# Lending the scan's PSUM banks, keeping a weight for two groups, and opening with zeros, in a two-layer kernel planned by a list scheduler

## The chip, the cores and the metric

The kernel runs on one core of a Trainium2 chip. The metric is the device time of one execution in microseconds (us). Three executions of the kernel before took 1812.67, 1815.26 and 1815.69 us, so the median is 1815.26 us. Everything is computed in float32.

The core has five engines that run their own instruction streams and meet at semaphores. In the profile PE is TensorE (matmuls; PEld is its loading of the stationary operand), DVE is VectorE, ACT is ScalarE, POOL is GpSimd, and SP only issues DMA transfers. A q behind an engine's name (SPq, POOLq, ACTq) is its instruction queue, most often while it issues a DMA.

## The reference

Two layers, each a sequence mixer and a feed-forward net (FFN), work on 2048 tokens of 512 features, with a residual and a layer norm behind every part:

```python
x = _layernorm(x + _L0_attn_ref(x, ...))   # chunked linear attention, 16 heads, decay per head
x = _layernorm(x + _L0_ffn_ref(x, ...))    # silu(x W1') * (x W3'), Walsh-Hadamard transform, W2'
x = _layernorm(x + _L1_attn_ref(x, ...))   # selective scan, 32 states a channel
x = _layernorm(x + _L1_ffn_ref(x, ...))    # silu(gate) * up, down projection

# L0 attention: q, k, v = silu(x Wq), silu(x Wk), silu(x Wv); per chunk of 128 tokens:
scores = einsum(qb, kb) * D                # D: decay by distance, causal
o = einsum(scores, vb) + einsum(qb, S) * q_decay
S = chunk_decay * S + einsum(kb * k_decay, vb)
# then sigmoid gate, RMS norm by head, Wo
# L1 scan over time, for each channel d and state n:
h = exp(delta_t * A) * h + (delta_t * u_t) * B_t;  y_t = sum_n h * C_t;  y + u * D_param
```

## The kernel before

**Groups and phases.** The tokens are worked in five groups (`GROUPS`): 256 tokens, three times 512, and 256. `PHASES` lists the work of the groups: `V0`..`V4` are the value products of the attention (`front`), `A0`..`A4` the rest of the attention (`attention`), `F0`..`F4` the first layer's FFN, and `f0, a1, b1, f2, f3, f4` the second layer's FFN. Between `F` and the small-letter phases lies the group's selective scan (class `Scan`). `F0`, `f0`, `a1` and `b1` (the phases named in `FILLERS`) run as fillers behind other work.

**Who sets the order.** Nothing is reordered by a compiler: the context is traced under a manual schedule. The class `Order` is a list scheduler that runs while the program is built. Every piece of work is an `Op` with an engine, a modelled duration, the buffers it reads and writes, the tagged buffers it takes and those it gives back. Each phase is a thread (a Python generator) that yields ops. `Order.run` takes for every engine the op that can begin first, with ties broken by a priority, and issues it. So each engine's instruction order is fixed by the model, and on the chip each engine follows that order and waits at semaphores. A thread can also yield a condition (`yield lambda: ...`); it goes on once that holds in the model.

**PSUM.** The eight banks are split for the whole run. Tag `mm` is four buffers of one bank, which all products, transposes and accumulations take in turn. Tag `da` is two buffers of two banks, which only the scan uses: ACT writes exp(delta A) there (L1412), DVE runs the scan in place (L1440) and multiplies by C (L1453).

**Weights.** `load_weights` streams all weights through a ring of 16 buffers of 256 KB each on SP's queue, in the order `PLAN`. Every phase takes its own pieces (`take`), so `Wv` is loaded once for each of the five groups. At piece 12 (3\*EB) and piece 28 (7\*EB) the stream stops until two, and then four, of the 1 MB quarters of W2 (`w2f`) have been requested. `transformed_w2` requests them; DVE and PE transform them and `w2h` in DRAM takes the result, which `F` phases read.

**The start.** `load_first` issues on SP: the identity matrix (needed by PE's transposes), the first group's two chunks of x, and then spawns the constants' loads (`load_consts`, all on POOL's queue, the decay parameters `ld` among the first), the weights and W2. Group 0: transposes (L527), copies out of PSUM (ACT, L534), value products (L607), q and k products (L658) in two blocks, gates (L677).

**The attention of later groups.** In `attention`, `projections` (the q and k products, L658) begin for groups 1 to 4 only when every chunk's values have been through their silu in the model (L970). The silu runs on ACT (L501), which must load another activation table (1.28 us, ACT_TABLE_LOAD) when it comes from exp or log work.

**The scan.** `Scan.inputs` transposes the group, and the product with W_bc (L1254) and the dt product (L1271) follow. `Scan.decays` issues the exps on ACT into `da`, `Scan.steps` the scans on DVE; `products` and `sums` run on POOL and by accumulating DMAs. Group after group: a scan begins its exps once the one before has issued its own.

Of the kernel before, what the change touches and what calls it, by code (L numbers as in the profile page):

```python
# [16 lines left out]
P = 128  # L17
# [25 lines left out]
FILLERS = {"F0": (), "f0": ("F0", "F1"), "a1": ("f0", "F2"), "b1": ("a1", "F3")}  # L43

PLAN = (
    "V0 A0 V1 A1:8 F0:8 A1 F0 F1 V2 A2:8 f0:8 A2 f0 F2 V3 A3:8 a1:8 A3 a1 F3 V4 A4:8 b1:8 A4 b1 "
    "F4 f2 f3 f4"
).split()

# [26 lines left out]
        self.r, self.w, self.a, self.free, self.spare = r, w, a, free, spare  # L76


class Order:


# [16 lines left out]
        self.now = 0.0  # L98

    def tag(self, name, n, make):  # L100
        self.tags[name] = (n, make, [])

    def spawn(self, gen, prio=0):
        self.new.append([gen, prio, None])
# [1 line left out]
    def begin(self, op, spare=True):  # L106

        t = self.free[op.eng]
        for b in op.r:
            if b.written is None:  # L110
                return None
            t = max(t, b.written + self.HOP)
        for b in op.w:
            t = max(t, b.last + self.HOP)
        for name in {name for name, _ in op.a}:
            n, _, bufs = self.tags[name]
            k = sum(name == v for v, _ in op.a) + (op.spare if spare else 0) - (n - len(bufs))
            if k > 0:
                free = sorted(b.last for b in bufs if b.refs <= 0)
                if len(free) < k:  # L120
                    return None
                t = max(t, free[k - 1] + self.HOP)
        return t

    def switches(self, op):
# [2 lines left out]

    def put(self, op, t):
        for name, b in op.a:  # L130
            n, make, bufs = self.tags[name]
            if len(bufs) == n:
                bufs.remove(min((v for v in bufs if v.refs <= 0), key=lambda v: v.last))
            b.t = make()
            bufs.append(b)
# [77 lines left out]
def two_layers(  # L213
# [15 lines left out]
    ps = ctx.enter_context(tc.tile_pool(name="ps", bufs=4, space=PSUM))  # L229
# [11 lines left out]
    def tagged(name, n, pool, shape):  # L241
        order.tag(name, n, lambda: pool().tile(shape, F32, tag=name, name=name, bufs=n))

    tagged("mm", 4, lambda: ps, [P, 512])
    tagged("da", 2, lambda: ps, [P, 2, G])
    tagged("xT", 2, lambda: gp, [P, EB * G])
    tagged("xf", 1, lambda: gp, [P, EB * G // 2])
    tagged("h", 10, lambda: gp, [P, G])
# [80 lines left out]
    def plan():  # L329
        for ph in PHASES:  # L330
            mine = of_phase[ph] = []
            if ph[0] in "VA":
                for w in (wv,) if ph[0] == "V" else (wq, wk, wo):
                    mine.extend((v, Buf(), ()) for v in rows_of(w, 0, EB))
                continue
            if ph[0] == "F":
                wg, wu, u0, wd, needs = w1t, w3t, 0, w2h, w2h_b
            else:
                wg, wu, u0, wd, needs = wgut, wgut, FF, wdnt, ()
            r0 = 0  # L340
# [7 lines left out]
        at = dict.fromkeys(PHASES, 0)  # L348
# [6 lines left out]
        assert all(at[ph] == len(of_phase[ph]) for ph in PHASES)  # L355

    def load_weights():
        for i, (src, b, needs) in enumerate(pieces):
# [59 lines left out]
    ident_b, consts_b, decays_b, scan_b, early_b, hadamard_b = (Buf() for _ in range(6))  # L418

    def load_first():  # L420
        nc.vector.memset(one, 1.0)
        nc.vector.memset(eps, EPS)
        nc.vector.memset(eps4, 4.0 * EPS)
        yield dma(KB256 / 4, lambda: ident, lambda: consts[:, C_ID : C_ID + P], w=[ident_b])
        yield from load_x(0)
        spawn(load_consts())
        spawn(load_weights())
        spawn(transformed_w2())

    def load_consts():  # L430
        yield dma(
            65536, lambda: early[:, 0, :], lambda: consts[:, C_H : C_H + P], eng="POOL",
            w=[hadamard_b],
        )

        yield dma(8192, lambda: ldb, lambda: ld.partition_broadcast(P), eng="POOL")
        for j in range(HPB):
            yield dma(
                512, lambda: ldp[j * HD : (j + 1) * HD, :],
                lambda: ld.rearrange("(k j) -> j k", j=HPB)[j].partition_broadcast(HD),  # L440
                allow_slow_non_contiguous=True, eng="POOL",
            )
        for j, c0 in ((1, C_DIFF), (2, C_MASK), (3, C_IDX)):
            yield dma(
                65536, lambda: early[:, j, :], lambda: consts[:, c0 : c0 + P],
                w=[early_b] if j == 3 else [], eng="POOL",
            )
        yield dma(
            4096, lambda: cst[:, 2 * P :], lambda: consts[:, C_REV : C_HM + 4],
            allow_slow_non_contiguous=True, eng="POOL",  # L450
        )
        yield dma(65536, lambda: blk, lambda: consts[:, C_BLK : C_BLK + P], eng="POOL")
        yield dma(65536, lambda: wg1_s, lambda: wg1.rearrange("(k p) e -> p k e", p=P), eng="POOL")
        for k in range(EB):
            yield dma(
                65536, lambda: wg2_s[k * HD : (k + 1) * HD, :], lambda: wg2, eng="POOL"
            )
# [167 lines left out]
    def attention(gi, nxt, prio):  # L625
# [341 lines left out]
        def projections():  # L967
            if gi:

                yield lambda: all(b.written is not None for b in v2)  # L970
            for vb in range(VB):
                for j in range(2):
                    yield from project(j, vb)
                if vb == 0:
                    yield from gates()
            reached(f"A{gi}")
# [236 lines left out]
    class Scan:  # L1213
# [189 lines left out]
        def decays(self):  # L1403
            if self.gi:
                yield lambda: scans[self.gi - 1].decayed
            U = len(self.units)
            for i, (n, k0) in enumerate(self.units):
                da, delta = self.da[i], self.delta[k0 // self.W]
# [19 lines left out]
        def steps(self):  # L1428
# [3 lines left out]
            for i, (n, k0) in enumerate(units):  # L1432
# [227 lines left out]
```

## Time and profile before

| what | value |
|---|---|
| median of three executions | 1815.26 us |
| the profiled execution's own span, first to last instruction | 1815.4 us |
| mean granted TensorE clock over it | 0.988 |
| PE busy | 1771.1 us (98%) |
| DVE, ACT, POOL busy | 1282.1, 1163.7, 1096.7 us |
| HBM traffic over the span | 152 GB/s |
| first and last exp of a scan (L1412) | 289.2 and 1663.3 us |
| transfers of 256 KB of Wv, median issue to landing | 20, 5.0 us |

The page gives each engine's busy time, the span in 40 slices, the chain of work that ended last, and the costliest groups. The waits view lists, for each line, whom it waited for: total, times, longest. The timeline gives one row for each merged run of instructions: start, duration, engine, line, what it writes and reads, count, and in brackets the idle time of the engine before it with what ended that idle time. The windows view gives, for each stretch, the busy time of the engines (in brackets their instructions), then the mean granted TensorE clock, the busy share of the DMA engines and GB/s.

### The profile page before, as it was taken

How to read it: one execution, taken by the hardware profiler on the slowest of the kernel's cores; microseconds unless marked ns; L12 is line 12 of the kernel's file. 1: busy time of each engine (PE TensorE's matmuls, PEld its weight loads, DVE VectorE, ACT ScalarE, POOL GpSimd, SP SyncE). 2: the span in 40 equal slices, each digit the busy share in tenths (PEclk: the TensorE clock that was granted, in tenths of full speed). 3: DMA queues.
4: the chain of work that ended last, by engine and by line, in shares of the span. 5: the costliest groups of instructions: out<-in, count | busy, mean ns of one | idle time of the engine just before them, and what ended most of it. 6: DMA issues, size and time to landing. Idle time of an engine off the chain costs nothing.

```text
span 1815.4 us, 21241 instructions
## 1 busy us (share of the span) xinstructions
PE 1771.1 (98%) x7064; PEld 1004.1 (55%) x7064; DVE 1282.1 (71%) x1537; ACT 1163.7 (64%) x1832; POOL 1096.7 (60%) x595
## 2 busy tenths in 40 slices
PE   8999999998999999999999999999999999999998
PEld 5456764443467644444666444676865444544574
DVE  3643115987599899944899999539999899998211
ACT  3734046688876676869767767686766868775311
POOL 2000015887577899935779989337998998776000
PEclk9999999999999999999999999999999999999999
DMA  9542435766648778745587787467989874766251
GB/s 283 156 139 82 151 118 168 197 164 175 210 128 253 206 207 233 200 119 185 154 221 221 199 231 212 143 213 236 275 241 262 204 213 159 199 172 168 81 174 58
DMA packets 225421, 336.32 MB, mean 185 GB/s; under 512 B 19569, under 2 KB 128897, under 8 KB 225313
## 3 DMA queue, kind: packets, MB, share of 16 engines
q1 hardware_dynamic: 206192, 270.86, 47.2%
q0 software_dynamic: 16816, 59.92, 17.6%
q10 hardware_dynamic: 2304, 4.20, 0.6%
q8 instruction: 56, 0.92, 0.2%
q14 instruction: 53, 0.43, 0.1%
HBM read 253.12 MB, written 22.54 MB: 152 GB/s over the span
## 4 chain that ended last, share of the span: by engine, by line
PE 67%; DVE 10%; ACT 8%; DMA 7%; POOL 4%; issue 3%; SPq 1%; DVEq 0%; POOLq 0%
PE mm L1052 36%; PE mm L1106 17%; DVE da L1440 6%; PE mm L658 4%; DMA y<-dbu 4%; POOL dbu L1392 3%; PE mm L1003 2%; ACT da L1412 2%; DVE dbu L1453 2%; PE mm L607 2%; ACT L501 1%; ACT L1412 1%; PE mm L845 1%; PE mm L1254 1%; PE mm L936 1%
## 5 line engine op out<-in xcount | busy, mean ns | idle before, releaser
L1392 POOL TENSOR_TENSOR dbu<-du,B 128x1024 f32<-128x1024 f32 x256 | 649.6, 2561 | 124.2 <-DMA y<-dbu 92.8
L1052 PE MATMUL mm<-xT,w 128*128 128x512 f32 (+1 forms) x1912 | 668.1, 510 | 2.9 <-ACT h L501 2.5
L1052 PEld LDWEIGHTS mm<-xT,w 128*128 128x128 f32 x1912 | 363.6, 191 | 303.9 <-issue 266.3
L1412 ACT ACTIVATE da<-delta,a_s 128x512 f32<-128x512 f32 (+1 forms) x640 | 384.4, 605 | 148.2 <-DVE dbu L1453 117.7
L1440 DVE TENSOR_TENSOR_SCAN da<-da,hlast,dbu 128x512 f32<-128x512 f32 (+1 forms) x384 | 425.8, 1109 | 36.9 <-ACT da L1412 27.7
L1489 POOL TENSOR_TENSOR y<-y,dbu 128x1024 f32<-128x1024 f32 x123 | 323.6, 2631 | 55.2 <-DVE dbu L1453 49.7
L1106 PE MATMUL mm<-w,h 128*128 128x512 f32 x768 | 339.4, 595 | 3.5 <-DMA w<-w2h 1.8
L1453 DVE TENSOR_TENSOR dbu<-da,C 128x1024 f32<-128x1024 f32 x256 | 312.9, 1222 | 13.9 <-ACT hlast L1465 7.0
L1440 DVE TENSOR_TENSOR_SCAN da<-da,dbu 128x256 f32<-128x256 f32 (+1 forms) x256 | 246.0, 961 | 26.7 <-ACT da L1412 18.8
L1106 PEld LDWEIGHTS mm<-w,h 128*128 128x128 f32 x768 | 145.2, 191 | 177.2 <-issue 164.4
L1052 PE MATMUL mm<-xf,w 128*128 128x256 f32 x1024 | 231.2, 385 | 0.2 <-DVE sc L863 0.2
L1052 PEld LDWEIGHTS mm<-xf,w 128*128 128x128 f32 x1024 | 196.7, 194 | 33.2 <-issue 4.6
L501 ACT ACT_TABLE_LOAD x143 | 183.5, 1283 | 5.1 <-PE mm L1052 2.3
L501 ACT ACTIVATE h<-mm 128x512 f32<-128x512 f32 x144 | 85.7, 597 | 114.3 <-PE mm L1052 66.3
L1083 DVE TENSOR_TENSOR h<-h,mm 128x512 f32<-128x512 f32 x96 | 65.2, 679 | 111.2 <-PE mm L1052 105.7
L1412 ACT ACT_TABLE_LOAD x109 | 139.8, 1283 | 1.9
L658 PE MATMUL mm<-xT,w 128*128 128x512 f32 (+1 forms) x320 | 116.6, 513 | 3.8 <-DVE sc L863 1.3
L299 POOL DMA_DIRECT2D y<-dbu x113 | 109.1, 966 | 12.4 <-DMA y<-dbu 5.1
L1465 ACT COPY hlast<-da 128x2 f32<-128x2 f32 (+1 forms) x160 | 25.4, 159 | 141.0 <-DVE dbu L1453 120.5
L1106 PE MATMUL mm<-w,hf 128*128 128x512 f32 x256 | 112.8, 592 | 0.0
L748 POOL TENSOR_TENSOR qd<-h,q_dec 128x512 f32<-128x512 f32 x14 | 17.8, 1271 | 151.0 <-ACT h L501 83.0
L1125 DVE TENSOR_TENSOR xn<-mm,xn 128x512 f32<-128x512 f32 x60 | 40.9, 681 | 92.9 <-PE mm L1106 92.5
(100 smaller groups left out, 1358.2 us busy)
## 6 DMA issues: line engine op xcount, KB each, us to landing
y<-dbu POOLq DMA_DIRECT2D x113, 512.0 KB, 6.0
w<-in_wgut_dram SPq DMA_DIRECT2D x192, 256.0 KB, 4.6
B<-rows SPq DMA_DIRECT2D x128, 256.0 KB, 4.6
C<-rows SPq DMA_DIRECT2D x128, 256.0 KB, 4.2
w<-in_wdnt_dram SPq DMA_DIRECT2D x96, 256.0 KB, 4.8
w<-in_w1t_dram SPq DMA_DIRECT2D x80, 256.0 KB, 4.7
w<-in_w3t_dram SPq DMA_DIRECT2D x80, 256.0 KB, 5.0
w<-w2h SPq DMA_DIRECT2D x80, 256.0 KB, 4.2
```

What stands on the lines that cost most here:

```text
L299: return Op(eng, us, lambda: of.dma_start(dst(), src(), **more), dma=nbytes, **kw)
L501: nc.scalar.activation(dst, src, AF.Silu)
L658: nc.tensor.matmul(bank.t[:, s * T : (s + 1) * T], w_qk[j][k].t[:, eb * P : (eb + 1) * P], xT.t[:, k, :], start=k == 0, stop=k == EB - 1,)
L1052: nc.tensor.matmul(bank.t[:, s * T + c0 * P : s * T + c1 * P], blocks[fb // 2][j][k // 2].t[:, k % 2 * 2 * P + k0 : k % 2 * 2 * P + k0 + P ...
L1083: 512, lambda: nc.vector.tensor_mul(t.t, t.t, pu.t), r=[pu], w=[t], free=[pu]
L1106: nc.tensor.matmul(accs[c].t, hT[f // S].t[:, s * T + c * P : s * T + (c + 1) * P], w_d[f].t, start=f == 0, stop=f == nt * S - 1,)
L1125: nc.vector.tensor_add(xb.t, bank.t, xb.t)
L1392: 1024, lambda: nc.gpsimd.tensor_mul(self.wide(self.db[i]), self.wide(du), self.row(self.bs, i)),
L1412: nc.scalar.activation(d[:, j, :], self.wide(delta)[:, j, :], AF.Exp, scale=a_s[:, k0 + j, n : n + 1],)
L1440: nc.vector.tensor_tensor_scan(d()[:, j, :], d()[:, j, :], self.wide(db)[:, j, :], init, ALU.mult, ALU.add,)
L1453: 1024, lambda: nc.vector.tensor_mul(self.wide(db), d(), self.row(self.cs, i)),
L1489: 1024, lambda: nc.gpsimd.tensor_add(y.t, y.t, db[i].t), r=o, w=[y],
```

## The change

The change has four parts, all in the planned program.

1. **Banks.** PSUM is now two tiles of four banks, and a new class `Banks` hands out single banks (`mm`) or aligned pairs (`da`) by when they come free. While no scan is open, `mm` may take all eight; while one is open it may take banks 0 to 3. A scan opens when its first `delta` load has been issued in the model and the scan before has issued its exps; it closes when its last multiplication has been issued.
2. **Wv for two groups.** `V1` leaves `PLAN`, and group 1 uses group 0's four buffers of Wv, which are held for both. The stop at piece 28 now falls behind four pieces of `F0`.
3. **The start.** DVE clears `dp1` (128x512), and PE multiplies zeros: one product of 512 and one of 256 columns at the very start, and one of 512 columns after the loads of x. The identity is issued on ACT's queue instead of SP's. The five small loads of `ld` go behind the gate weights in POOL's queue.
4. **q and k.** The condition at L970 becomes one that always holds, so q and k products no longer stand behind the values' silu.

```diff
 PLAN = (
-    "V0 A0 V1 A1:8 F0:8 A1 F0 F1 V2 ..."
+    "V0 A0 A1:8 F0:8 A1 F0 F1 V2 ..."
...
+class Banks:
+    def __init__(self, views, usable):
+        self.views, self.usable = views, usable
+        self.holders = [None] * 8
+    def free_at(self, i):
+        b = self.holders[i]
+        return -1.0 if b is None else b.last if b.refs <= 0 else None
...
+class BankTag:
+    def places(self):
+        f, out = self.banks.free_at, []
+        for i in self.banks.usable(self.width):
+            at = [f(j) for j in range(i, i + self.width)]
+            if None not in at:
+                out.append((max(at), i))
+        return sorted(out)
...
-    tagged("mm", 4, lambda: ps, [P, 512])
-    tagged("da", 2, lambda: ps, [P, 2, G])
+    halves = [ps.tile([P, 4, G], F32, name=name) for name in ("mm", "da")]
+    opened = set()
+
+    def usable(width):
+        if width == 2:
+            return (4, 6)
+        return range(4 if opened else 8)
...
+            if ph == "V1":
+                for v, b, needs in of_phase["V0"]:
+                    b.refs += 1
+                    mine.append((v, b, needs))
+                continue
...
     def load_first():
+        nc.vector.memset(dp1, 0.0)
...
-        yield dma(KB256 / 4, lambda: ident, lambda: consts[:, C_ID : C_ID + P], w=[ident_b])
+        spawn(warming(3.0, (512, 256)))
+        yield dma(
+            KB256 / 4, lambda: ident, lambda: consts[:, C_ID : C_ID + P], eng="ACT", w=[ident_b]
+        )
         yield from load_x(0)
+        spawn(warming(0.9, (512,)))
...
+    def warming(us, cols):
+        bank = Buf()
+        def mm():
+            for n in cols:
+                nc.tensor.matmul(
+                    bank.t[:, :n], dp1[:, :P], dp1[:, :n], start=True, stop=True
+                )
+        yield pe(us, mm, a=[("mm", bank)], free=[bank])
...
     def load_consts():
...
-        yield dma(8192, lambda: ldb, lambda: ld.partition_broadcast(P), eng="POOL")
-        for j in range(HPB):
-            yield dma(512, lambda: ldp[j * HD : (j + 1) * HD, :], ..., eng="POOL")
...
         for k in range(EB):
             yield dma(65536, lambda: wg2_s[k * HD : (k + 1) * HD, :], lambda: wg2, eng="POOL")
+        yield dma(8192, lambda: ldb, lambda: ld.partition_broadcast(P), eng="POOL")
+        for j in range(HPB):
+            yield dma(512, lambda: ldp[j * HD : (j + 1) * HD, :], ..., eng="POOL")
...
         def projections():
             if gi:
-                yield lambda: all(b.written is not None for b in v2)
+                yield lambda: True
...
         def decays(self):
             if self.gi:
                 yield lambda: scans[self.gi - 1].decayed
+            yield lambda: self.delta[0].written is not None
+            opened.add(self.gi)
...
             self.stepped = True
+            opened.discard(self.gi)
```

More of the change, by code (lines that the diff above doesn't have):

```diff
@@ L45 @@
 PLAN = (
-    "V0 A0 V1 A1:8 F0:8 A1 F0 F1 V2 A2:8 f0:8 A2 f0 F2 V3 A3:8 a1:8 A3 a1 F3 V4 A4:8 b1:8 A4 b1 "
+    "V0 A0 A1:8 F0:8 A1 F0 F1 V2 A2:8 f0:8 A2 f0 F2 V3 A3:8 a1:8 A3 a1 F3 V4 A4:8 b1:8 A4 b1 "
     "F4 f2 f3 f4"
@@ L76, in __init__, with when, take, of @@
         self.r, self.w, self.a, self.free, self.spare = r, w, a, free, spare
+class Tiles:
+    def __init__(self, n, make):
+        self.n, self.make, self.bufs = n, make, []
+    def when(self, k):
+        k -= self.n - len(self.bufs)
+        if k <= 0:
+            return -1.0
+        free = sorted(b.last for b in self.bufs if b.refs <= 0)
+        return free[k - 1] if len(free) >= k else None
+    def take(self, b):
+        if len(self.bufs) == self.n:
+            self.bufs.remove(min((v for v in self.bufs if v.refs <= 0), key=lambda v: v.last))
+        b.t = self.make()
+        self.bufs.append(b)
+class Banks:
[5 more added lines that the diff above has]
+        return -1.0 if b is None else b.last if b.refs <= 0 else None
+    def of(self, width):
+        return BankTag(self, width)
+class BankTag:
+    def __init__(self, banks, width):
+        self.banks, self.width = banks, width
+    def places(self):
[5 more added lines that the diff above has]
+        return sorted(out)
+    def when(self, k):
+        free = self.places()
+        return free[k - 1][0] if len(free) >= k else None
+    def take(self, b):
+        at, i = self.places()[0]
+        b.t = self.banks.views(i, self.width)
+        for j in range(i, i + self.width):
+            self.banks.holders[j] = b
 class Order:
@@ L100, in tag @@
     def tag(self, name, n, make):
-        self.tags[name] = (n, make, [])
+        self.tags[name] = Tiles(n, make)
     def spawn(self, gen, prio=0):
@@ L115, in begin @@
         for name in {name for name, _ in op.a}:
[L116 to L122, printed above, removed]
+            k = sum(name == v for v, _ in op.a) + (op.spare if spare else 0)
+            free = self.tags[name].when(k)
+            if free is None:
+                return None
+            t = max(t, free + self.HOP)
         return t
@@ L130, in put @@
         for name, b in op.a:
[L131 to L135, printed above, removed]
+            self.tags[name].take(b)
         op.fn()
@@ L228, in two_layers @@
     sm = ctx.enter_context(tc.tile_pool(name="sm", bufs=12))
-    ps = ctx.enter_context(tc.tile_pool(name="ps", bufs=4, space=PSUM))
+    ps = ctx.enter_context(tc.tile_pool(name="ps", bufs=1, space=PSUM))
     dr = ctx.enter_context(tc.tile_pool(name="dr", bufs=1, space=DRAM))
@@ L242, in tagged, with views @@
         order.tag(name, n, lambda: pool().tile(shape, F32, tag=name, name=name, bufs=n))
-    tagged("mm", 4, lambda: ps, [P, 512])
-    tagged("da", 2, lambda: ps, [P, 2, G])
+    halves = [ps.tile([P, 4, G], F32, name=name) for name in ("mm", "da")]
[4 more added lines that the diff above has]
+        return range(4 if opened else 8)
+    def views(i, width):
+        half = halves[i // 4]
+        return half[:, i % 4, :] if width == 1 else half[:, i % 4 : i % 4 + width, :]
+    banks = Banks(views, usable)
+    order.tags["mm"], order.tags["da"] = banks.of(1), banks.of(2)
     tagged("xT", 2, lambda: gp, [P, EB * G])
@@ L347, in plan @@
                 r0 += blocks * P
-        at = dict.fromkeys(PHASES, 0)
+        at = dict.fromkeys((ph for ph in PHASES if ph != "V1"), 0)
         for v in PLAN:
@@ L354, in plan @@
             at[ph] += n
-        assert all(at[ph] == len(of_phase[ph]) for ph in PHASES)
+        assert all(n == len(of_phase[ph]) for ph, n in at.items())
     def load_weights():
@@ L434, in load_consts @@
         )
-        yield dma(8192, lambda: ldb, lambda: ld.partition_broadcast(P), eng="POOL")
-        for j in range(HPB):
[L438 to L442, printed above, removed]
         for j, c0 in ((1, C_DIFF), (2, C_MASK), (3, C_IDX)):
@@ L456, in load_consts @@
                 65536, lambda: wg2_s[k * HD : (k + 1) * HD, :], lambda: wg2, eng="POOL"
+            )
+        yield dma(8192, lambda: ldb, lambda: ld.partition_broadcast(P), eng="POOL")
+        for j in range(HPB):
+            yield dma(
+                512, lambda: ldp[j * HD : (j + 1) * HD, :],
+                lambda: ld.rearrange("(k j) -> j k", j=HPB)[j].partition_broadcast(HD),
+                allow_slow_non_contiguous=True, eng="POOL",
             )
```

## The prediction

> **What bounds the kernel now.** First the page's busy times and its chain of work that ended last, by engine:
>
> ```profile
> PE 1771.1 (98%) x7064; PEld 1004.1 (55%) x7064; DVE 1282.1 (71%) x1537; ACT 1163.7 (64%) x1832; POOL 1096.7 (60%) x595
> PE 67%; DVE 10%; ACT 8%; DMA 7%; POOL 4%; issue 3%; SPq 1%; DVEq 0%; POOLq 0%
> ```
>
> PE is the bound. No matmul of the program goes away, so only two things can be won: PE's idle time, 1815.4 - 1771.1 = 44 us, and the time in which its clock is halved. The mean granted clock is 0.988, so that is about 0.012 x 1815 = 22 us. About 7 us of the idle time is the tail behind the last matmul (layer norm and store), which the change leaves alone. Then PE's waits, and its rows in the timeline of the first 45 us:
>
> ```profile
> PE mm L1254 <- ACT xT L534: 6.6, 2, 3.6
> PE mm L527 <- DMA xn<-in_x_dram: 4.4, 1, 4.4
> PE mm L607 <- DMA w<-in_wv_dram: 4.0, 2, 2.4
> ```
>
> ```profile
> 4.45 1.98 PE L527 MATMUL mm<-cst,xn 128*128 128x128 f32 x8 [4.45 <-DMA xn<-in_x_dram]
> 7.99 9.27 PE L607 MATMUL mm<-w,xT 128*128 128x512 f32 x16 [1.57 <-DMA w<-in_wv_dram]
> 21.76 2.87 PE L658 MATMUL mm<-xT,w 128*128 128x256 f32 x12 [0.18 <-DMA w<-in_wk_dram]
> 36.01 5.37 PE L607 MATMUL mm<-w,xT 128*128 128x512 f32 x8 [2.39 <-DMA w<-in_wv_dram]
> ```
>
> The two longest kinds of wait are for data at the start and for ACT's copies before L1254. The value products of groups 0 and 1 are slow too: 8 rows at 36.01 take 5.37 us, and 8 such rows elsewhere take 3.60. The weight loads show the clock at 12 us:
>
> ```profile
> 11.54 0.34 PEld L607 LDWEIGHTS mm<-w,xT 128*128 128x128 f32 x1 [0.52 <-issue]
> 12.38 0.19 PEld L607 LDWEIGHTS mm<-w,xT 128*128 128x128 f32 x1 [0.50 <-issue]
> ```
>
> So PE runs at about half speed until 12.4 us. The windows view gives DMA rates and the granted clock (the last three columns are clock, DMA share, GB/s):
>
> ```profile
> 0.00:10.00 10.00, 3.99 (x11) 2.39 (x12) 0.12 (x3) 3.74 (x4) 6.39 (x15) 1.00 0.57 165
> 10.00:20.00 10.00, 10.00 (x29) 5.50 (x28) 0.00 (x0) 3.27 (x6) 3.53 (x6) 1.00 0.90 288
> 30.00:40.00 10.00, 7.61 (x29) 4.80 (x28) 8.48 (x8) 1.56 (x3) 0.00 (x0) 0.83 1.03 366
> 433.00:445.00 12.00, 8.30 (x16) 3.73 (x17) 9.57 (x13) 10.40 (x18) 6.97 (x5) 0.72 0.78 225
> 800.00:812.00 12.00, 8.85 (x22) 3.90 (x21) 2.99 (x8) 9.04 (x20) 0.08 (x1) 0.86 0.34 109
> ```
>
> A gap costs its length and a slow stretch behind it: at 33.6 to 36.0 us 2.39 us idle and 10 x 0.17 = 1.7 us of clock; at 433 to 445 us 3.61 idle and 12 x 0.28 = 3.4; at 800 to 812 us 3.00 and 12 x 0.14 = 1.7. Last, the timeline at the second of these:
>
> ```profile
> 437.35 6.21 PE L1254 MATMUL mm<-xT,wbc 128*128 128x512 f32 x8 [3.61 <-ACT xT L534]
> 438.98 1.28 ACT L501 ACT_TABLE_LOAD   x1
> 440.28 0.60 ACT L501 ACTIVATE h<-mm 128x512 f32<-128x512 f32 x1
> 443.40 3.60 PE L658 MATMUL mm<-xT,w 128*128 128x512 f32 x8
> ```
>
> Here PE stands idle until 437.35, while the first q product of group 2 (L658) waits for its place behind the last silu of the values, 440.28. At 803.3 to 806.3 the order is the same: the last values' silu is at 808.56, L658 at 811.58.
>
> **The change, part by part.** *The start.* The identity leaves SP's queue, where it takes 0.43 us ahead of x (0.74 to 1.17), so x and all weights are issued 0.43 us sooner. On ACT's queue it stands before or behind the first table load (1.28 us): at worst it lands near 4.3 us (2.0 + 0.4 of issue + 1.9 to land), about when x does now, so this is -0.43 to +0.3. I take -0.4. The memset of dp1 is bounded by the small memsets (0.06) and by a DVE op on 128x512 (0.69); DVE has nothing else before 20.5 us. The zeros are two and later one product. Each is two rows of 0.85 us (512 columns) at the slow clock, all while PE would wait for x (4.45) and Wv (1.57). If that cover were gone they would cost up to 4 us. They should make the clock full by 8 us instead of 12.4: (12.4 - 8) / 2 = 2.2 us.
>
> But the first group is not PE's alone. K's weights let PE begin at 21.76 only, and PE reaches that point with no slack to speak of (0.18 waited). A faster V0 just makes that wait longer, unless Wk lands sooner. The five `ld` loads now lie at 2.0 to 4.8 us on POOL's queue, and the later constants wait for them there (5.5 us in all). While they are under way the DMA engines move 165 GB/s, afterwards 288. If they are the cause, loads up to 10 us lack about 0.65 MB of what the later rate would bring, worth 2.3 us; put later they slow Wk or W2 instead. So Wk comes 0.4 to 2.7 us earlier; I take 1.4, between the two, since the slow stretch is moved rather than removed. Moved behind the gate weights, `ld` delays the decays on ACT (19.2 us) by up to the 5.5 us they cost others; these are not read by PE's work before 43 us.
>
> *Wv for two groups.* Four transfers of 256 KB leave the queue, and with them the wait of 2.39 us and its clock loss of 1.7. What is late next is x of group 1, which PE transposes at 32.14, and PE's own q and k products, which end at 32.3 (less 1.4). So V1 begins near 32.5 instead of 36.0: 3.5 us, plus 1.7 of clock, is 5.2; the 0.51 us at 45.6 (DVE's scores) may go or stay. Bounds: if PE idles before Wk long enough to fall to the slow clock again, 1.7 is lost and 3.5 stay; with everything early, 3.5 + 1.7 + 1.3 + 0.5 = 7. I take 5.5 for the start as a whole. The ring buffers held longer push F0's first pieces and the last two W2 quarters, now at 39.9, behind V1 (near 60 us). Their butterflies (16 x 1.22 us of DVE) and products move with them; F0 reads w2h from 154 us on and the last store is at 109 us, so some 25 us of cover remain. Gone, the cost would be PE's wait for L1106.
>
> The Trainium skill (TensorE: Matmul & The Clock Gate, Part 1) says that PE warms only after about 3.4 us of sustained work and cools only after an idle window of about that length. By that rule the gap of 2.39 us need not cool PE, and the zeros alone (2.6 us) need not warm it. The rows disagree on the first point: the clock fell after 2.39 us. By the rule the start would be worth 3.8 instead of 5.5.
>
> *q and k.* The wait on a silu goes at 433.7 and 803.3. A q product is 3.43 us of PE work and its weights were requested at 388 and 757. Filled, the gaps are worth 3.61 + 3.4 = 7.0 and 3.00 + 1.7 = 4.7. What is late next: the other waits of the same attention, 0.35 to 1.08 us each between 469 and 504 (4.9 us together), where the q and k products now fill gaps. Taken earlier, they are missing there. Each silu also needs ACT's tables switched twice (2.56 us) between the scan's exps. So the gain lies between 0 (all given back) and 11.7; I take half, 5.5, since half of the q and k products are left as filler.
>
> *Banks.* PE's waits that a DVE or ACT reader of a bank ends (L863, L778 rows) sum to 5.6 us, and nearly all lie where a scan is open or about to open. Before 285 us they are 0.7. So lending is worth 0 to 1 us: 0.5. The cost is that a scan's first exp must wait until lent banks are read out: one silu or copy, 0.6 us, at five openings, off PE's path. It needs cover, and there is some: the last scan ends at 1669.7, and behind it PE still has work of other groups (L1106 rows) mixed into the last FFN:
>
> ```profile
> 1702.21 3.45 PE mm L1052 x16
> 1705.66 6.87 PE mm L1106 x16
> 1740.06 41.44 PE mm L1052 x192
> 1781.50 27.48 PE mm L1106 x64
> ```
>
> From 1698.8 to 1740 these L1106 rows make 3.4 + 3 x 6.9 + 3.4 = 27.5 us. The scans may end that much later before PE starves.
>
> **Sum.** 5.5 + 5.5 + 0.5 = 11.5 us off 1815.4, the profiled span, which stands 0.1 us over the median of the runs: 1804 us.
>
> **The rivals.** *The start alone* (chance 0.27): q and k only move their waits, and the result is 1815 - 6 = 1809. For it speak the six shorter waits in the same stages. *DMA hides the start as well* (0.12): Wk and x of group 1 stay where they are, PE idles before L658 at 20 us and cools, and only about 2 us come out: 1813. For it speaks that DMA works at 288 to 366 GB/s from 10 to 40 us. Against it: 1 MB less stands ahead of V1. *Slower* (0.15): products taken early put silus between the exps of an open scan. ACT is busy 10.40 of 12 us at 433 to 445, and each silu with its two switches costs 3.2 us. The copies that L1254 needs come later still, and new gaps appear in each of groups 1 to 4. One like that at 437 us costs 7 us; three of them, less 11.5 in gains that would be 5.5 without the q and k part, give 1815 - 6 + 21 = 1830, two give 1823. It decides from the first: 6 us of start are eaten by one such gap. Against it speaks that PE has waits of 2 us or more only four times behind 40 us now (3.61, 3.00, 2.03, 2.51). I price it at 1823.
>
> **How the numbers follow.** The forecast has 0.46 (1798 to 1808 by its own bounds). Executions differ by 3 us, so about 0.2% (3.6 us) can be told from no change: below 1811.6 is faster, above 1818.9 slower. Forecast and first rival are faster, 0.73, with a little of the second, 0.75; the rest of it is the same, 0.10; slower 0.15. The range runs from 1795, all bounds taken well, to 1818, which leaves out most of the slower case.
>
> **What would show it.** Right: the row of L607 with 2.39 us of idle gone, V1 at about 32.5; weight loads of 0.19 us at the first L607 row; L658 at 434 and 803 ahead of L1254, the granted clock there near 1.00. Wrong: a wait of L658 for Wk of over 2 us with loads of 0.34 behind it; L1254 or L845 waiting longer in the stages at 440 to 520 and 800 to 890; a last scan past 1697.

## The result and the profile after

| | before | after |
|---|---|---|
| median, five executions each | 1815.26 us | 2677.39 us |
| profiled span | 1815.4 us | 2677.9 us |
| mean granted clock | 0.988 | 0.914 |
| first and last exp of a scan | 289.2, 1663.3 us | 344.5, 2530.1 us |

The changed kernel takes 1.4765 times as long, interval [1.4744, 1.4786]. The prediction was 1804 us with a range to 1818; it is wrong by 873 us and in sign.

The line numbers of the changed kernel are higher: L607 is now L694, L658 is L745, L1052 is L1139, L501 is L588, L1083 is L1170; the scan's exp L1412, scan L1440, product with C L1453 and copy L1465 are L1501, L1529, L1542 and L1555. In the kernels of the experiments they lie up to nine lower or three higher than in the changed kernel; tiles and operations tell which is which. Busy times of the page and its chain by engine, after:

```profile
PE 2027.0 (76%) x7070; PEld 1058.7 (40%) x7070; DVE 1312.0 (49%) x1538; ACT 1174.0 (44%) x1830; POOL 1101.7 (41%) x595
PE 11%; DVE 11%; ACT 7%; issue 1%; DMA 0%; POOL 0%; DVEq 0%; ACTq 0%; POOLq 0%
```

The instruction counts are those of before but for the six rows of zeros, one memset and two ACT rows fewer, and DVE, ACT and POOL are busy for only 5 to 30 us more (1282, 1164 and 1097 us before). PE was the bound at 98%; now no engine is. The chain could be followed back only to 1840.7 us, 31% of the span; in that part PE and DVE have about a third each and ACT a fifth, where PE had 67% of the chain before. Of the 862.5 us of span, 606.6 are PE's idle time (2677.9 - 2027.0 = 650.9, against 44.3) and 255.9 are longer PE rows. The clock accounts for most of the second part: the trace's record of the granted clock shows 86 stretches at half clock, 462 us in all, where before had ten, 47 us in all. Half of PE's busy time in these stretches, 192 us after and 19 us before, is an estimate of what they cost. The other 83 us of longer rows were not traced.

Who waits for whom, from the waits view of after (total, times, longest):

```profile
ACT da L1501 <- DVE da L1529: 443.8, 239, 6.3
POOL y L1579 <- DVE dbu L1542: 423.0, 116, 13.7
DVE da L1529 <- ACT da L1501: 403.5, 277, 15.5
...
PE mm L1139 <- ACT h L588: 135.3, 69, 5.0
PE mm L1139 <- DVE h L1170: 73.2, 70, 2.4
```

The same pair of waits before:

```profile
DVE da L1440 <- ACT da L1412: 46.5, 53, 4.0
...
ACT da L1412 <- DVE da L1440: 14.2, 13, 1.9
```

At L1052, which is now L1139, PE waited before only once for a silu (2.5 us) and never for L1083. In the changed kernel the exp waits for the scan *and* the scan for the exp, over 200 times each, although the scan has two buffers. The timeline of after shows it (first row: a scan of one `da` buffer; second: an exp that fills the other):

```profile
1502.71 1.28 DVE L1529 TENSOR_TENSOR_SCAN da<-da,hlast,dbu 128x512 f32<-128x512 f32 x1
...
1504.03 0.69 ACT L1501 ACTIVATE da<-delta,a_s 128x512 f32<-128x512 f32 x1 [2.67 <-DVE da L1529]
1504.75 1.22 DVE L1542 TENSOR_TENSOR dbu<-da,C 128x1024 f32<-128x1024 f32 x1 [0.76 <-ACT da L1501]
1506.01 0.16 ACT L1555 COPY hlast<-da 128x2 f32<-128x2 f32 x1 [1.29 <-DVE dbu L1542]
...
1507.92 0.60 ACT L588 ACTIVATE h<-mm 128x512 f32<-128x512 f32 x1
1508.57 3.70 PE L1139 MATMUL mm<-xT,w 128*128 128x512 f32 x8 [2.03 <-ACT h L588]
...
1512.31 0.69 DVE L1170 TENSOR_TENSOR h<-h,mm 128x512 f32<-128x512 f32 x1
1513.05 3.70 PE L1139 MATMUL mm<-xT,w 128*128 128x512 f32 x8 [0.78 <-DVE h L1170]
```

Each engine starts within 0.05 us of the other's end: the exp at 1504.03 when the scan has ended (1503.99), the product with C at 1504.75 when the exp has (1504.72). The FFN has it too. PE begins a product at 1508.57, when the silu of another product's bank has ended (1508.52), then computes 3.7 us while neither ACT nor DVE reads `mm`, and begins the next at 1513.05, when DVE has read a bank (1513.00). In the program that the kernel builds, that silu reads bank 2 and the product that waits for it writes bank 0; DVE reads bank 3 and the product that waits for it writes bank 1. Four banks behave like one buffer.

The start, which the prediction worked on, looks as intended. The PE rows of after:

```profile
1.46 2.93 PE L511 MATMUL mm<-dp 128*128 128x512 f32 x4 [1.46 <-DVE eps L494]
...
7.78 7.03 PE L694 MATMUL da<-w,xT 128*128 128x512 f32 x16
15.49 3.72 PE L745 MATMUL da<-xT,w 128*128 128x256 f32 x16 [0.69 <-ACT h L588]
...
34.53 3.70 PE L694 MATMUL mm<-w,xT 128*128 128x512 f32 x8 [0.29 <-ACT xT L621]
```

The zeros run from 1.46 us, the first 16 value rows take 7.03 instead of 9.27 us (2.24 us less; the prediction had 2.2 for the clock), and V1 begins at 34.53 instead of 36.01. But here too PE waits for a silu (0.69 at 15.49). The slow rows at the start show in the durations alone: the record of the granted clock has 1.00 there before too. Windows of after (clock, DMA share and GB/s in the last columns) no longer show the slow clock in the third stretch, where before had 0.83:

```profile
10.00:20.00 10.00, 8.62 (x29) 4.88 (x27) 0.00 (x0) 1.33 (x3) 2.95 (x6) 1.00 0.93 268
30.00:40.00 10.00, 9.02 (x70) 5.70 (x68) 9.10 (x9) 3.99 (x8) 0.00 (x0) 1.00 0.95 318
```

### The profile page after: what moved, and what is told of

Read it like the earlier page. It is cut to its first block, busy times and chain, and to the rows that moved or that the text cites. A ratio compares the mean times of both kernels' runs of the same rounds, so it can differ in the third digit from the quotient of the medians.

```text
span 2677.9 us, 21522 instructions
## 1 busy us (share of the span) xinstructions
PE 2027.0 (76%) x7070; PEld 1058.7 (40%) x7070; DVE 1312.0 (49%) x1538; ACT 1174.0 (44%) x1830; POOL 1101.7 (41%) x595
## 3 DMA queue, kind: packets, MB, share of 16 engines
q0 software_dynamic: 16816, 59.92, 11.6%
## 5 line engine op out<-in xcount | busy, mean ns | idle before, releaser
L1139 PE MATMUL mm<-xT,w 128*128 128x512 f32 (+1 forms) x1720 | 705.6, 559 | 242.1 <-ACT h L588 135.3
L1479 POOL TENSOR_TENSOR dbu<-du,B 128x1024 f32<-128x1024 f32 x256 | 627.6, 2463 | 60.6 <-DMA du<-dd 48.3
L1501 ACT ACTIVATE da<-delta,a_s 128x512 f32<-128x512 f32 (+1 forms) x640 | 387.8, 606 | 511.7 <-DVE da L1529 443.8
L1139 PEld LDWEIGHTS mm<-xT,w 128*128 128x128 f32 x1720 | 334.4, 202 | 611.1 <-issue 230.7
L1529 DVE TENSOR_TENSOR_SCAN da<-da,hlast,dbu 128x512 f32<-128x512 f32 (+1 forms) x384 | 427.2, 1112 | 260.4 <-ACT da L1501 237.8
L1579 POOL TENSOR_TENSOR y<-y,dbu 128x1024 f32<-128x1024 f32 x123 | 288.5, 2346 | 456.4 <-DVE dbu L1542 423.0
L1542 DVE TENSOR_TENSOR dbu<-da,C 128x1024 f32<-128x1024 f32 x256 | 313.1, 1223 | 103.8 <-ACT da L1501 92.8
L1529 DVE TENSOR_TENSOR_SCAN da<-da,dbu 128x256 f32<-128x256 f32 (+1 forms) x256 | 246.8, 964 | 188.8 <-ACT da L1501 165.7
L1139 PE MATMUL mm<-xf,w 128*128 128x256 f32 x912 | 244.9, 429 | 62.7 <-ACT hf L588 20.0
L1193 PEld LDWEIGHTS mm<-w,h 128*128 128x128 f32 x672 | 136.8, 210 | 267.2 <-issue 155.4
L1139 PEld LDWEIGHTS mm<-xf,w 128*128 128x128 f32 x912 | 193.8, 217 | 118.4 <-ACT hf L588 25.7
L364 POOL DMA_DIRECT2D y<-dbu x113 | 98.5, 872 | 289.7 <-DVE dbu L1542 278.8
L1170 DVE TENSOR_TENSOR h<-h,mm 128x512 f32<-128x512 f32 x91 | 62.1, 683 | 193.4 <-PE mm L1139 150.6
L1555 ACT COPY hlast<-da 128x2 f32<-128x2 f32 (+1 forms) x160 | 25.7, 161 | 232.3 <-DVE dbu L1542 157.5
L1193 PE MATMUL mm<-w,hf 128*128 128x512 f32 x224 | 106.2, 622 | 24.3 <-DVE xn L1212 12.6
L588 ACT ACTIVATE h<-mm 128x512 f32<-128x512 f32 x121 | 72.1, 597 | 115.8 <-PE mm L1139 47.0
L745 PE MATMUL mm<-xT,w 128*128 128x512 f32 (+1 forms) x208 | 97.4, 622 | 15.4 <-DVE sc L950 6.5
L614 PE MATMUL mm<-cst,xn 128*128 128x128 f32 x212 | 38.0, 315 | 70.7 <-ACT h L588 24.2
```

The costliest lines, as they stand in the source:

```text
L364: return Op(eng, us, lambda: of.dma_start(dst(), src(), **more), dma=nbytes, **kw)
L588: nc.scalar.activation(dst, src, AF.Silu)
L614: nc.tensor.transpose(bank.t[:, db * P : (db + 1) * P], xn[gi, c].t[:, db * P : (db + 1) * P], ident,)
L745: nc.tensor.matmul(bank.t[:, s * T : (s + 1) * T], w_qk[j][k].t[:, eb * P : (eb + 1) * P], xT.t[:, k, :], start=k == 0, stop=k == EB - 1,)
L1139: nc.tensor.matmul(bank.t[:, s * T + c0 * P : s * T + c1 * P], blocks[fb // 2][j][k // 2].t[:, k % 2 * 2 * P + k0 : k % 2 * 2 * P + k0 + P ...
L1170: 512, lambda: nc.vector.tensor_mul(t.t, t.t, pu.t), r=[pu], w=[t], free=[pu]
```

## The experiments

**Theory.** The two PSUM tiles cause the loss. Before, `mm` was four tiles of one bank and `da` two tiles of two. The change allocates `halves`, two tiles of four banks, and gives out slices. If the program's waits are set for a tile and not for a bank, an access waits for other engines' accesses to neighbouring banks. **Rivals:** the lending itself (a scan waits for lent banks, PE for the scan's), or the replanned order (zeros, Wv, q and k).

How often waits cross banks can be counted in the programs that the kernels build (not in a trace): each wait of PE, ACT or DVE on another of them was resolved to the instruction that releases it, and those were counted where the two instructions share a PSUM tile but no bank. A wait that the program puts into an instruction of its own counts for the next one of that engine.

| kernel | PSUM tiles (in banks) | waits across banks of a tile / all | us |
|---|---|---|---|
| before | 1,1,1,1,2,2 | 237 / 2152 | 1815.3 |
| after | 4,4 | 1932 / 2458 | 2677.4 |
| before's order, tiles merged | 4,4 | 2078 / 2532 | 2929.8 |
| after's order, tiles split | 1,1,1,1,2,2 | 348 / 2100 | 1802.3 |
| the same, `da` merged | 1,1,1,1,4 | 996 / 2454 | 2276.8 |
| the same, `mm` merged | 4,2,2 | 1349 / 2079 | 2373.7 |
| the same, `mm` in pairs | 2,2,2,2 | 949 / 1921 | 1914.0 |

Of the 237 of before, 216 are scans that wait for the exp of the other half of their own pair. The expectation for the pairs below works with lower counts (117, 845 and 568); with those of the table its sum gives 2145 instead of 2160 us.

### Only the merged tiles

Everything but the tiles is as before: no lending, no zeros, Wv for each group, the wait at the q and k products. The order on every engine is that of before.

```diff
-    tagged("mm", 4, lambda: ps, [P, 512])
-    tagged("da", 2, lambda: ps, [P, 2, G])
+    halves = [ps.tile([P, 4, G], F32, name=name) for name in ("mm", "da")]
...
+    def views(i, width):
+        half = halves[i // 4]
+        return half[:, i % 4, :] if width == 1 else half[:, i % 4 : i % 4 + width, :]
```

> The kernel before with one edit: the four mm banks are views of one PSUM tile and the two da pairs are views of another. No lending, weights, start and q, k as before; each engine's instructions stand in the same order as before. Theory A (an engine's access to a PSUM tile is made to wait for the other engines' accesses to any bank of that tile, so one tile of four banks works as one bank): about 2700 us, 2500 to 2900, with PE waiting for silus that read another bank and ACT's exps for DVE's scans. Theory B (lending, or the new order of the work, is what slows it): within 0.3% of 1815 us.

Measured: 2929.78 us, ratio 1.6154 [1.6114, 1.6195], just over the expected range. The same pair of waits stands first and third (waits view of this kernel):

```profile
ACT da L1492 <- DVE da L1520: 452.5, 237, 8.8
...
DVE da L1520 <- ACT da L1492: 361.4, 276, 11.3
```

The merge alone does the whole damage and more; neither lending nor order is needed for it.

### The changed kernel with split tiles

```diff
-    halves = [ps.tile([P, 4, G], F32, name=name) for name in ("mm", "da")]
+    single = [ps.tile([P, G], F32, name=f"mm{i}") for i in range(4)]
+    double = [ps.tile([P, 2, G], F32, name=f"da{i}") for i in range(2)]
...
-        half = halves[i // 4]
-        return half[:, i % 4, :] if width == 1 else half[:, i % 4 : i % 4 + width, :]
+        if i < 4:
+            return single[i]
+        pair = double[(i - 4) // 2]
+        return pair[:, i % 2, :] if width == 1 else pair
```

> The changed kernel with one edit: banks 0 to 3 are four tiles of one bank, banks 4 to 7 two tiles of two, as before; lending, weights, start and q, k stay changed and each engine's instructions stand in the changed kernel's order. Theory A: the time falls from 2677 to about what the parts are worth, 1804 us (1795 to 1818 as predicted). Theory B: it stays near 2677, since order and lending are untouched.

Measured: 1802.3 us, ratio 0.9935 [0.9918, 0.9951]. The instructions and their order on each engine are those of the changed kernel; only the waits differ, and 875 us go. The exp's wait for the scan is 14.8 us again, the scan's for the exp 61.4. Busy times, then rows of the timeline in which ACT fills one `da` buffer while DVE multiplies the other by C, and PE goes on through both:

```profile
PE 1758.6 (98%) x7070; PEld 997.8 (55%) x7070; DVE 1283.2 (71%) x1538; ACT 1161.4 (64%) x1830; POOL 1096.9 (61%) x595
```

```profile
1384.47 9.60 PE L1142 MATMUL mm<-xT,w 128*128 128x512 f32 x22
...
1385.35 0.60 ACT L591 ACTIVATE h<-mm 128x512 f32<-128x512 f32 x1
...
1386.67 0.67 DVE L1173 TENSOR_TENSOR h<-h,mm 128x512 f32<-128x512 f32 x1
...
1387.26 1.21 DVE L1545 TENSOR_TENSOR dbu<-da,C 128x1024 f32<-128x1024 f32 x1
1387.26 1.42 ACT L1504 ACTIVATE da<-delta,a_s 128x512 f32<-128x512 f32 x2
```

The Trainium skill (Perfetto Trace Analysis, Optimizing Tensor Performance) advises to rotate independent products through different banks, so that ACT and DVE empty one during the next product. The two kernels rotate through the same banks in the same order; only with split tiles does the overlap come, 1802 against 2677 us.

So the loss is the tiles, and what is left of the change is a gain of 0.65%. That it lies within 2 us of the forecast is luck, as the parts below show.

### One tile merged at a time, and pairs

From the split kernel, either banks 4 to 7 become one tile again, or banks 0 to 3 do, or these become two tiles of two.

```diff
-    double = [ps.tile([P, 2, G], F32, name=f"da{i}") for i in range(2)]
+    shared = ps.tile([P, 4, G], F32, name="da")
...
```

> The changed kernel with mm as four tiles, da still one tile of four banks. Theory A: the scan alone works in turn (exp, then scan, then exp); its five runs took 2197 us from first exp to last in the changed kernel against 1380 before, and it sets the time: 2400 to 2650 us, with PE waiting little for silus. Theory B: near 2677.

```diff
-    single = [ps.tile([P, G], F32, name=f"mm{i}") for i in range(4)]
+    shared = ps.tile([P, 4, G], F32, name="mm")
...
```

> The changed kernel with da as two tiles of two banks, mm still one tile of four. Theory A: PE waits for the silu or the multiplication of the product before (135 + 73 + 24 + 23 us and more in the changed kernel), the scan runs as before: 2100 to 2400 us. Theory B: near 2677.

```diff
-    single = [ps.tile([P, G], F32, name=f"mm{i}") for i in range(4)]
+    single = [ps.tile([P, 2, G], F32, name=f"mm{i}") for i in range(2)]
...
```

> Banks 0 to 3 as two tiles of two banks (in the kernel with split tiles they are four tiles, 1802.3 us; as one tile of four, 2373.7 us); all else as in the kernel with split tiles. Theory (each wait that the program sets on an instruction of another bank of the same tile costs time): the built program has 568 of these waits, where the kernel with split tiles has 117 and the one with one tile of four banks 845, so 1802 + (451 / 728) x 571 = about 2160 us, 2000 to 2250. By the number of banks that share a tile alone (one neighbour in place of three) it would be 1802 + 571 / 3 = 1992 us. Rival (it is the one tile of four banks, or the address of the banks, that hurts): near 1802, or near 2374.

Measured, one execution each: 2276.81, 2373.71 and 1913.99 us; the first is faster than its range, the second inside it, the third near none of its values. Each merged tile brings back its own waits. Waits view with `da` merged, then with `mm` merged:

```profile
ACT da L1503 <- DVE da L1531: 383.2, 244, 4.6
DVE da L1531 <- ACT da L1503: 368.5, 322, 7.3
```

```profile
PE mm L1142 <- ACT h L591: 61.2, 59, 3.1
PE mm L1142 <- DVE h L1173: 60.2, 70, 1.5
...
ACT da L1504 <- DVE da L1532: 11.6, 9, 2.9
```

The exp that waits for the scan is at 383 us with `da` merged and at 11.6 with `mm` merged. Alone they cost 475 and 571 us, together 875, less than their sum. The pairs were expected at 2160 us from the count of waits, or 1992 from the number of neighbours; they cost only 112 us. So the direction holds, but there is no one price per wait: 0.73 and 0.57 us for each added wait of the table in the two merged kernels, 0.19 in the pairs. That with two tiles an engine mostly finds its next bank in the other one is likely, but it was only argued.

### A control, and the parts one by one

All of these have the split tiles. The control takes the new class of banks with before's order; the others add to it one part of the change each: the start with Wv for two groups, the q and k products, the lending.

```diff
-        return range(4 if opened else 8)
+        return range(4)
...
-            yield lambda: self.delta[0].written is not None
             opened.add(self.gi)
```

This takes the lending out. The next one takes the q and k part out:

```diff
-                yield lambda: True
+                yield lambda: all(b.written is not None for b in v2)
```

The start is taken out by undoing parts 2 and 3 of the change as its diff shows them.

> The control to the run with the merged tiles: the kernel before, its four mm banks and two da pairs handed out through the new class, but as six tiles of their own; the same instructions in the same order on every engine and in the same banks as that run. If only the waits that a shared tile brings make it slow, this is within 0.3% of 1815 us; if the new class or the choice of banks does (theory B in another form), it is far above.

> The kernel before with split tiles and only the start and Wv changed (zeros, identity on ACT's queue, ld loads later, Wv for two groups); no lending, q and k behind the silu. As predicted the start is worth 5.5 us (3.5 to 7): 1808 to 1812 us. Rival (the start is hidden by DMA): 2 us or less, 1813 to 1816.

> Split tiles, no lending, start as before, only the q and k condition changed. As predicted 5.5 us, half of the two gaps of 7.0 and 4.7: 1808 to 1813 us. Rivals: given back in later waits, 1815; or silus between the exps of an open scan, 1820 and more.

> Split tiles, start and q, k as before, only the lending of banks. As predicted 0 to 1 us: 1814 to 1816 us. Rival: free banks let PE run ahead where no scan is open and fill the waits of the attention, 1805 to 1811 us.

> Split tiles, no lending: the parts start (zeros, identity, Wv for two groups, late ld loads) and q, k products together. Alone they are worth 2.7 us and 15.8 us. Theory (the start moves PE's work of the first 430 us ahead by 4 to 6 us, and the gaps behind are then filled by the q and k products): additive, 1815 - 2.7 - 15.8, near 1797, 1793 to 1800. Rival (what the parts gain is lost where the last group's scan opens, as in the kernel with all three): 1800 to 1805.

> Split tiles, lending and the q, k products together, the start as before. Alone they are worth 9.6 us and 15.8 us. Theory (the two meet where the fourth and fifth groups' scans open: in the kernel with all three parts PE waits 4.8 us for a silu at 1398.9 us, behind an exp, where the kernel with the q, k products alone has no such wait): 1800 to 1805, no faster than the q, k products alone. Rival (additive): 1815 - 9.6 - 15.8 = 1789 to 1791.

> Split tiles, the start and lending together, the q and k products behind the values' silu as before. Alone they are worth 2.7 us and 9.6 us. Theory (lending fills PE's waits for banks in all groups, the start moves the first 430 us; they don't meet): additive, 1815 - 2.7 - 9.6, 1801 to 1805. Rival (each moves the same idle time of PE): 1804 to 1809.

The gain is (1 - ratio) times the median of before in the same runs, 1813 to 1814 us.

| parts | median us | ratio to before | gain us |
|---|---|---|---|
| none (control) | 1815.37 | 1.0003 [0.999, 1.0017] | 0 |
| start | 1811.85 | 0.9985 [0.9972, 0.9998] | 2.7 |
| q, k | 1798.29 | 0.9913 [0.9898, 0.9928] | 15.8 |
| lending | 1804.21 | 0.9947 [0.9934, 0.996] | 9.6 |
| start, q, k | 1792.11 | 0.989 [0.9875, 0.9905] | 19.9 |
| start, lending | 1793.21 | 0.9892 [0.9875, 0.9908] | 19.6 |
| lending, q, k | 1810.81 | 0.9992 [0.9981, 1.0002] | 1.5 |
| all three | 1802.30 | 0.9935 [0.9918, 0.9951] | 11.8 |

The control shows no cost of the new class beyond 0.2%. Only the control and the start lie in the range of their theory, the start at its upper edge. The start with q, k comes near its sum (18.5 expected, 19.9 measured). The other sums fail, in both directions: lending with q, k gives 24 us less than apart, more than the clash that was expected, and start with lending 7 us more, which neither expectation had. The best versions are the split tiles with the start and either the q, k products or the lending, 1.1% faster than before; between these two the intervals do not decide.

Where the parts act can be followed in the timelines, by the start of each group's first W_bc product (L1254 before) and the end of the last matmul. These are single executions; two kernels with the same instructions in the same order (before and its control) differ by 2 to 5 us in them.

| parts | group 0 | 1 | 2 | 3 | 4 | last matmul ends |
|---|---|---|---|---|---|---|
| control | 253.8 | 435.4 | 803.4 | 1168.7 | 1390.1 | 1804.4 |
| start | 249.9 | 431.5 | 801.0 | 1167.6 | 1389.3 | 1804.7 |
| q, k | 254.6 | 436.2 | 797.6 | 1154.0 | 1374.9 | 1789.9 |
| lending | 261.7 | 443.3 | 808.2 | 1175.3 | 1386.3 | 1802.2 |
| start, q, k | 250.7 | 432.3 | 791.6 | 1148.1 | 1368.7 | 1783.1 |
| start, lending | 248.6 | 430.2 | 795.0 | 1162.0 | 1373.1 | 1786.6 |
| lending, q, k | 258.7 | 440.3 | 809.9 | 1156.9 | 1376.6 | 1800.9 |
| all three | 248.3 | 429.9 | 799.1 | 1149.4 | 1369.0 | 1795.1 |

*Start alone* (against the control): 3.9 us ahead at group 0 and still at group 1, 2.4 at group 2, 0.8 at group 4, nothing at the end. V1 in fact begins 5.2 us earlier than before (36.01), and Wk is waited for, but at full clock (timeline, PE):

```profile
19.54 2.43 PE L748 MATMUL mm<-xT,w 128*128 128x256 f32 x10 [1.47 <-DMA w<-in_wk_dram]
...
30.80 3.70 PE L697 MATMUL mm<-w,xT 128*128 128x512 f32 x8
```

*q and k:* both gaps go. The products with W_bc, by line and form, first before and then with the q, k part alone (busy us, mean ns, idle before):

```profile
L1254 PE MATMUL mm<-xT,wbc 128*128 128x512 f32 x24 | 15.3, 797 | 6.6 <-ACT xT L534 6.6
```

```profile
L1336 PE MATMUL mm<-xT,wbc 128*128 128x512 f32 x24 | 11.1, 604 | 0.5 <-ACT xT L616 0.5
```

The idle time falls by 6.1 us and the busy time by 4.2 us (each of the 24 rows is 193 ns shorter, and rows overlap): 10.3 us at these rows alone. Nothing is given back at 440 to 600 us (PE busy 155.9 against 154.7 of 160 us). By group 3 the lead over the control is 14.7 us, and it stays (14.5 at the end).

*Lending:* 7.9 us behind the control at groups 0 and 1, ahead by 3.8 at group 4. From 45 to 285 us PE is busy for 234.1 us, in the kernel before for 238.9, and there are slow stretches of the clock at 113.7 and 181.9 us; with the start added these are not there, and group 0 is 13.1 us earlier. What it gains behind that is not idle time, of which it has more (46.8 us, control 43.5): PE's rows are 5.5 us shorter in all (1761.8 against 1767.3). Why they are shorter was not found out. This profiled execution took 1810.8 us and is the longest of the six of this kernel, so it shows little of the 9.6 us. The other five (1803.5 to 1804.7 us) had a mean granted clock of 0.992 to 0.995; this one had 0.989, the control's eight 0.988 to 0.992. By the medians, 0.993 and 0.989, up to 0.004 x 1810 = 7 us of the gain may be clock; this is an estimate, and no trace of those five is there to show which stretches they were spared.

*Lending with q, k:* most of the lead of q, k at group 3 is kept (1156.9) and lost at the end: from the start of group 4's W_bc to the last matmul this kernel takes 424.3 us and that with all three parts 426.1, the other six 413.5 to 415.9. Waits view of this kernel:

```profile
PE mm L1134 <- ACT h L583: 4.8, 1, 4.8
...
PE da L927 <- ACT h L583: 2.6, 1, 2.6
PE mm L811 <- ACT h L583: 2.4, 3, 1.3
...
PE mm L848 <- ACT h L583: 1.8, 1, 1.8
```

These 11.6 us of waits for a silu are there with all three parts too (4.8, 2.6, 2.0 and 1.8). With the lending alone none of the four shows, and the q, k part alone has 1.9 us of the first and none of the rest. The longest, in this kernel's timeline:

```profile
1402.09 0.42 ACT L1394 ACTIVATE th<-pt 128x256 f32<-128x256 f32 x1 [4.65 <-POOL pt L1406]
...
1405.69 0.60 ACT L583 ACTIVATE h<-mm 128x512 f32<-128x512 f32 x1
...
1406.34 1.97 PE L1134 MATMUL mm<-xT,w 128*128 128x512 f32 x2 [4.80 <-ACT h L583]
```

ACT waits 4.65 us for POOL before the softplus of the scan's dt, and the silu that gives PE its bank stands behind it. Before has a wait of that length at this line too (4.3 us), but PE's one wait for a silu at the FFN is 2.5 us there; with the q, k part alone it is 3.9 and 1.9. So ACT's wait alone does not make the loss, and what in the order does is not shown. The four kinds of wait make somewhat under half of the 24 us; the rest was not traced.

## Why the prediction was wrong

**Banks: the step that failed.** The prediction said "lending is worth 0 to 1 us: 0.5. The cost is that a scan's first exp must wait until lent banks are read out: one silu or copy, 0.6 us, at five openings, off PE's path." The cost was looked for in who gets which bank, not in how the banks are allocated. The line with `halves` turns six tiles into two, and that costs 875 us with the same instructions in the same order. The prediction put its cost at nothing: no rival held it and no bound was set for it. The trace of before could not show two engines at different banks of one tile, except within a `da` pair, but a bound was to be had from its page: if ACT and DVE take turns at `da`, the exps (384 us) lie end to end with the scans and products with C (426 + 246 + 313 us) instead of beside them. That is 1369 us, as long as the 1374 us between the first and the last exp before: the scans would have had no slack left.

The lending itself, with split tiles, is worth 9.6 us and not 0.5. PE's waits for readers of a bank while no scan is open (0.7 us before 285 us) were taken for its size. But the planner makes another order of all that follows, so a gain need not lie where a wait was; part of it may be clock, as said above, and its cause stays open.

**q and k: the mechanism right, the term mis-sized.** L658 is ahead at both places (432.39 and 793.70 with this part alone) and both gaps go. The prediction took about half of 11.7 us, 5.5, because taken fillers would be missing at 469 to 504 us. They were not; 15.8 us came out, over its upper end. The lengths of the gaps were a better forecast than the discount; where the 4 us above them come from was not traced.

**Start: right in place, mis-sized at the end.** The wait of 2.39 us went, and V1 came at 30.8 us, ahead of the 32.5 predicted. By the medians it is worth 2.7 us alone against 5.5, although it is 5.2 us ahead at V1: the lead fades in later stages, and what takes it there was not traced. That "only about 2 us come out" (DMA hides the start) is the size, but not that rival's reason: PE waits 1.47 us for Wk and keeps the full clock. With other parts beside it the start is worth 4 (with q, k), 10 (with lending) and 10 us (with both).

**Sum.** With split tiles the forecast of 1804 meets 1802.3, but by luck, with terms whose errors cancel: 2.7, 15.8 and 9.6 us, 28.1 in all, instead of 5.5, 5.5 and 0.5, and 16 of them lost where the parts meet. **Slower** was right in sign for another reason: its mechanism, silus between exps that keep PE waiting, is worth at most 11.6 us where lending and the q, k products meet, and never decided.

The Trainium skill (TensorE: Matmul & The Clock Gate, Part 1) asks for an idle window of about 3.4 us before the clock falls. The traces do not agree: with all three parts and split tiles the half clock begins at 862.2 us, behind a single gap of 1.18 us.

## What to carry to other kernels

Read an allocation as part of the schedule: in these programs waits are set by tile, so banks that different engines use at a time belong in tiles of their own, and slices of one tile undo the double buffering that they seem to give. When two engines wait for each other hundreds of times and no engine is the bound, look for a shared buffer before looking at the order; splitting it while the order is held is a test that settles it. In a kernel planned by a scheduler, parts of a change do not add: measure each alone and in pairs, since each of the two best here leaves out one of three parts that each gain alone.

## What the runs showed that was not expected

PE's half clock is granted in stretches of about 3.4 us or a multiple of it (up to 13.7 us in the changed kernel; a stretch at the end of a trace is cut short), and it does not need one long gap: behind idle times of 1.0 to 2 us in all it fell in several places, while single gaps of 1.8 us at 472 and 2.3 us at 776 us (split tiles) were not followed by it. The same gap of 1.18 us that was followed by it with all three parts was not with lending and the q, k products (at 870.2 us). Its price shows in the rows of a line: 24 products with W_bc at 797 ns on average against 604 with the gap ahead of them filled. Of the 862 us by which the changed kernel's span is longer about 173 are this clock by the estimate above (192 against 19), a cost of waiting beyond the waits.
